# Two graph convolutions and an attention on 200,000 edges: attention by products in the second pass, bf16 parts, and three in-place copies of each one-hot block

## The chip, the core and the metric

The program runs on one core of a Trainium2 chip. A core has five engines that this text names: TensorE (PE: matmuls; PEld: its weight loads), VectorE (DVE), ScalarE (ACT), GpSimd (POOL, which issues the indirect DMAs, here gathers of rows by an index) and SyncE (SP, which issues plain DMAs). Each takes its own instructions strictly in order; they wait for each other by semaphores. The metric is the device time of one execution in microseconds (us). The kernel before takes 4932.1 us, the median of 23 runs from 4896.84 to 4955.6.

## What is computed

Cut to what matters (x is 12500 x 256, src and dst have 200,000 entries, dst is sorted):

```python
def _gcn_conv(x, W, b, src, dst, n):          # src, dst with a loop per node
    h = x @ W
    deg = segment_sum(ones, dst); dinv = rsqrt(deg)
    msgs = h[src] * (dinv[src] * dinv[dst])[:, None]
    return segment_sum(msgs, dst, num_segments=n) + b

def gcn(x):
    h = x @ W_pre + b_pre
    h = relu(_gcn_conv(h, W1, b1)); h = relu(_gcn_conv(h, W2, b2))
    return h @ W_post + b_post

def attention(x):                             # 4 heads x 64
    xt = (x @ weight).reshape(-1, 4, 64)
    alpha_l = einsum('ehd,hd->eh', xt[row], attn_l)
    alpha_r = einsum('ehd,hd->eh', xt[col], attn_r)
    alpha = softmax(leaky_relu(alpha_l + alpha_r, 0.01), axis=1)
    tmp = einsum('nh,nhd->nd', alpha[:n], xt[col[:n]])
    return broadcast tmp over the 4 heads     # n x 256

x = x + gcn(relu(layernorm(x)))
x = x + attention(relu(layernorm(x)))
```

The attention uses only the first 12500 edges (alpha[:n]), and as dst is sorted their targets are the first nodes of the graph (the first 9 windows of 128 nodes), while their sources may be any node.

## The kernel before

A general path for other inputs is not taken here. The fast path has four stages: preparation (to about 132 us: layer norm, degrees, the scaled table of rows in DRAM, table1), pass 1 and pass 2 over all edges, one for each graph convolution, and the attention's tail (from 4717 us). Nodes are in 98 windows of 128. Edges are in 112 chunks of 14 tiles of 128 edges, 1563 tiles in all.

Both passes are one function, `convolve` (L1153), called at L1437 over table1 and at L1597 over table2. For each tile:

- GpSimd gathers 128 source rows of 256 f32 values from the table into a slot of a chunk's buffer (L1374, `fgot`). Pass 1 has buffers for five chunks (the first four chunks of pass 1 need no gather), pass 2 for four. The buffer is free when the last product of the chunk that used it has ended.
- The one-hot block of the tile, 128 edges x 128 places of the target (`fhot`), is made by VectorE for a whole chunk, one chunk ahead (L1241).
- TensorE adds one-hot transposed times rows to the chunk's accumulator in PSUM (L1382, `facc`). One f32 product is two records in the profile.

When a chunk's last tile has been issued, `close` copies the accumulator by ScalarE (L1276, `fsums`), and schedules two steps: `turn`, eight tiles on, transposes the sums (L1206, `fturn`), and `add`, thirteen tiles on, adds them by VectorE to a sliding buffer of nodes at an offset read from memory (L1293, `buf`). When a window of 128 nodes is complete, `add` schedules the window's own steps. Their order is written out by hand: `at(t, step)` puts a step into a list with the tile after which it is issued, and `run(t)`, called after each tile, issues what is due. So the order on each engine is that of the program, and a step stands behind every tile's instructions issued before it.

A window's steps in pass 1 (`finish1`): a product with the weights (L1417, L1418, six tiles on), and ScalarE's relu to `fo` (L1422, ten tiles on), which is then stored to table2 by a DMA that ScalarE issues (L1423). In pass 2 (`finish2`): two products (`fpz`, L1472; `fpo`, L1488) with relu `fz` (L1482) between; the residual and the statistics of the second layer norm (L1493 to L1504; `sc`, L1501); the normalised rows `h` (L1509), their transposes (L1514, `fpt`), the copy `ht` (L1518), the product with the attention's weights (L1527, `fpx`) and its copy `fxa` (L1535). Parts of this are stored to small tables: `table_l`, `table_e` (left scores) and `table_r` (right rows of the first nine windows); the residual is kept in `kept_x`.

The tail mixes the attention's result for 98 tiles of 128 edges in groups of seven: a gather of left scores for each tile (L1662, `fal`), the right rows by one-hot products (L1652, `fends`), copied by ScalarE (L1654), products for scores not yet in a table (L1633, `lacks`), a softmax over the four heads on VectorE and ScalarE (L1666 to L1678), the weighted sum of heads (L1685 to L1692), and the addition to the kept rows (L1694, `fres`), stored to the output.

Of the kernel before, what the change touches and what calls it, by code (L numbers as in the profile page):

```python
# [17 lines left out]
P = 128  # L18
# [395 lines left out]
def fast_path(  # L414
# [57 lines left out]
    table2 = dram.tile([NT * P, D], F32, name="ftable2")  # L472
    kept_x = dram.tile([NT * P, D], F32, name="kept_x")
# [3 lines left out]
    assert AC * J == NT and AC * CE <= E and XW < NT  # L477
    table_r = dram.tile([XW * P, DR], F32, name="table_r")
    table_l = dram.tile([NT * P, H], F32, name="table_l")

    LW = 3
    table_e = dram.tile([NT * P, H], F32, name="table_e")
# [18 lines left out]
    base_b = const.tile([P, NCH], F32, name="base_b")  # L501
    row_i = const.tile([P, AC], I32, name="row_i")
# [88 lines left out]
    with tc.tile_pool(name="fprep", bufs=1) as prep:  # L591
# [233 lines left out]
        with tc.tile_pool(name="fpsum", bufs=2, space=PSUM) as psum, \  # L825
# [227 lines left out]
            wide = prep.tile([NCH, P], F32, name="wide")  # L1053
            nc.vector.tensor_copy(wide, base.to_broadcast([NCH, P]))
# [7 lines left out]
            nc.tensor.matmul(fk[:, 2, :NCH], wide, ident[:NCH, :NCH], start=True, stop=True)  # L1062
# [7 lines left out]
            for f in after:  # L1070
                f()
            after = [raw_block(ends, m, psum.tile([P, 4 * P], F32, name="ft"), j0)
                     for j0 in (8, 12)]
            nc.vector.tensor_copy(base_b, fk[:, 2, :NCH])
            nc.vector.tensor_scalar(row_i, base_b[:, :AC], lane, float(XW * P - 1), op0=ALU.add,
                                    op1=ALU.min)
# [16 lines left out]
    def check_chunks(work, psum):  # L1093
# [20 lines left out]
        kept = work.tile([1, 1], F32, name="n_kept", bufs=1)  # L1114
        nc.vector.tensor_reduce(kept, pt[:1, 2, :NCH], AX.X, ALU.add)
        nc.vector.tensor_add(kept, kept, counted)
        nc.vector.tensor_scalar(bad_row, kept, -1.0, float(NCH + 1), op0=ALU.mult, op1=ALU.add)
# [12 lines left out]
    def load_late(pool):  # L1130

        nc.scalar.dma_start(roots, root_t)
        for t, w in ((wb, w2), (wo, w_post), (wg[:, :, :D], w_gat)):
            nc.scalar.dma_start(t, w.rearrange("(k p) n -> p k n", p=P))
        nc.scalar.dma_start(b2c, b2.rearrange("(k p) -> p k", p=P))
        nc.scalar.dma_start(bob, b_post.partition_broadcast(P))
        attn = []
        for a in (attn_r, attn_l):
            ar = pool.tile([P, D], F32, name="far", bufs=2)
            nc.scalar.dma_start(ar, a.rearrange("h c -> (h c)").partition_broadcast(P))  # L1140
            attn.append(ar)
        return attn

    def late_weights(pool, attn):

        for i, ar in enumerate(attn):
            for k in range(KC):
                prod = pool.tile([P, H, C], F32, name="fprod", bufs=1)
                nc.vector.tensor_mul(prod.rearrange("p h c -> p (h c)"), wg[:, k, :D], ar)
                nc.vector.tensor_reduce(wg[:, k, D + i * H:D + (i + 1) * H], prod, AX.X,  # L1150
                                        ALU.add)

    def convolve(ep, table, stride, width, ahead, with_sum, psum, prepare, finish, lacking=False,  # L1153
                 raw=(), rows_p=None):
# [28 lines left out]
        def run(now=None):  # L1183

            while due:
# [3 lines left out]
                do(d)  # L1189

# [41 lines left out]
        const_p = psum.tile([P, P if with_sum else P + D], F32, name="iota_p", bufs=1)  # L1232
        iota_p = const_p[:, :P]
        nc.vector.tensor_copy(iota_p, iota_w)
        if not with_sum:
            state["bias"] = const_p[:, P:]
            nc.vector.tensor_copy(state["bias"], bob)

# [4 lines left out]

        def hot_of(c):

            n = nj[c]
            h = ep.tile([P, J, P], F32, name="fhot", bufs=3)
# [3 lines left out]
        def new_rows_of():  # L1251
            if with_sum:
                return new_got()
            return rows_p.tile([P, J, stride], F32, name="fgot", bufs=ahead)

        def late_sums():

            h = ep.tile([P, J, P], F32, name="fhot", bufs=3)
# [5 lines left out]
            px = psum.tile([P, KC, P], F32, name="fpt", bufs=1)  # L1264
# [75 lines left out]

        tiles = [(c, j) for c in range(NCH) for j in range(nj[c])]
# [23 lines left out]
        for t, (c, j) in enumerate(tiles):  # L1365
# [7 lines left out]
            if c >= len(raw):  # L1373
                nc.gpsimd.indirect_dma_start(  # L1374
                    out=got, out_offset=None, in_=table[:(NT - TW) * P, :] if some else table[:],
# [4 lines left out]
            if j == (5 if some else 2) and c + 1 < NCH:  # L1380
                hots[c + 1] = hot_of(c + 1)
            nc.tensor.matmul(acc, hots[c][:, j, :], got[:, :width], start=(j == 0),  # L1382
                             stop=(j == nj[c] - 1 and not some))
# [6 lines left out]
            if c + 1 < len(raw):  # L1390
                raw_ahead(c + 1, j)
            run(t)
        run()


# [14 lines left out]
    def finish1(work, psum, w, buf, sbuf, fs):  # L1410
# [9 lines left out]
        def e():  # L1420
            o = work.tile([P, D], F32, name="fo", bufs=3)
            nc.scalar.activation(o, v["po"], AF.Relu, scale=dinv2[:, w:w + 1])  # L1422
            nc.scalar.dma_start(table2[w * P:(w + 1) * P, :], o)  # L1423
            if w == 8:
                late_weights(late, attn)
                first_chunk()
            if w == 9:
                check_chunks(late, psum)

        return [(6, d, fills(w, "fpo")), (10, e, None)]  # L1430

    with tc.tile_pool(name="psum1", bufs=1, space=PSUM) as psum, \
# [6 lines left out]
                 rows_p=late)  # L1439
    ring.close()  # L1440

    ap = ctx.enter_context(tc.tile_pool(name="fatt", bufs=2))
    rows = [ap.tile([P, DR], F32, name="rows", bufs=AC) for c in range(AC)]
    EARLY = 2

    FROM = 40
    assert J % G == 0 and FROM > XW + 2 and FROM + J < NT - LW
    lates = {w: ap.tile([P, DA], F32, name="fxl", bufs=LW) for w in range(NT - LW, NT)}
    early = [ap.tile([P, G, DR], F32, name="fxe", bufs=J // G) for g in range(J // G)]
    hot_l = [ap.tile([P, CE], F32, name="hot_l", bufs=LW) for i in range(LW)]  # L1450

    def prepare2(work, w):
# [6 lines left out]
        nc.sync.dma_start(xb[:n, :], x[w * P:w * P + n, :])  # L1461
        return rb, xb

    def finish2(work, psum, w, buf, pre, bias):
        v = {"root": pre[0], "x": pre[1]}

        def d():
            pz = in_psum(psum, w, "fpz", [P, D], "facc", [P, D], 2)
# [16 lines left out]
        def f():  # L1485
            po = v["po"] = in_psum(psum, w, "fpo", [P, D], "facc", [P, D], 2)
# [4 lines left out]
        def g():  # L1491
# [9 lines left out]
            nc.scalar.activation(v["sc"], mv[:, 1:2], AF.Sqrt, bias=eps)  # L1501

# [8 lines left out]
        def i():  # L1511
            pt = v["pt2"] = in_psum(psum, w, "fpt", [P, KC, P], "fturn", [P, 2 * KC, P])
            for k in range(KC):
                nc.tensor.transpose(pt[:, k, :], v["h"][:, k * P:(k + 1) * P], ident)  # L1514

        def k():
            v["ht"] = work.tile([P, KC, P], F32, name="ht2")
            nc.scalar.activation(v["ht"], v["pt2"][:, :KC, :], AF.Copy)  # L1518
# [4 lines left out]
        def q():  # L1523
            px = in_psum(psum, w, "fpx", [P, DA], "iota_p", [P, P + D])
            px = v["px"] = px[:, d0:] if w + 1 < NT else px[:, :H]
# [4 lines left out]
        def r():  # L1530
            if w < NT - LW:
                xa = work.tile([P, DA], F32, name="fxa")
            else:
                xa = lates[w]
            nc.scalar.activation(xa[:, d0:], v["px"], AF.Copy)  # L1535
            nc.scalar.dma_start(table_l[w * P:(w + 1) * P, :], xa[:, DR:])
            if w < NT - LW:
                nc.scalar.dma_start(table_e[w * P:(w + 1) * P, :], xa[:, DR:])
            if w < XW:
                nc.scalar.dma_start(table_r[w * P:(w + 1) * P, :], xa[:, :DR])  # L1540

        steps = [(6, d, fills(w, "fpz")), (8, e, None), (12, f, fills(w, "fpo")), (14, g, None),
                 (16, h, None), (20, i, fills(w, "fpt")), (22, k, None),
                 (26, q, fills(w, "fpx")), (28, r, None)]
        t = w - FROM
        if 0 <= t < J:

            if t == 0:
                own_rows(0)

            def ends():
                px = v["ends"] = in_psum(psum, w, "fpx", [P, DA], None, None)[:, :DR]
                nc.tensor.matmul(px, hot_t[0][:, t * P:(t + 1) * P], rows[0], start=True,
                                 stop=True)

            def copied():
                nc.scalar.activation(early[t // G][:, t % G, :], v["ends"], AF.Copy)

            steps += [(32, ends, "fpx"), (34, copied, None)]
        return steps  # L1560


    hot_t = {}

    def load_ends(pool, c, bufs):
        to_all = pool.tile([P, CE], I32, name="to_all", bufs=bufs)
        nc.sync.dma_start(to_all, dst[c * CE:(c + 1) * CE].partition_broadcast(P))
        return to_all

    def turn_hots(pool, c, to_all, bufs):  # L1570
        hot_t[c] = pool.tile([P, CE], F32, name="hot_t", bufs=bufs)
        nc.vector.tensor_scalar(hot_t[c], to_all, base_b[:, c:c + 1], lane,  # L1572
                                op0=ALU.subtract, op1=ALU.is_equal)

    def own_rows(c):

        nc.gpsimd.indirect_dma_start(
            out=rows[c], out_offset=None, in_=table_r[:],
            in_offset=bass.IndirectOffsetOnAxis(ap=row_i[:, c:c + 1], axis=0))

    with tc.tile_pool(name="psum2", bufs=1, space=PSUM) as psum, \
            tc.tile_pool(name="fwork2", bufs=2) as work, \
            tc.tile_pool(name="edges2", bufs=1) as ep, \
            tc.tile_pool(name="fgots2", bufs=1) as rows_p:
        ep.tile([P, 320], F32, name="apart")
        for c in range(EARLY):
# [166 lines left out]
```

## Time and profile before

| | |
|---|---|
| median of 23 runs | 4932.1 us (4896.84 to 4955.6) |
| the profiled execution | 4923.27 us |
| its span | 4921.3 us |
| TensorE, matmul records | 2709.2 us, 55% |
| TensorE, weight loads | 2070.9 us, 42% |
| VectorE | 1140.6 us, 23% |
| ScalarE | 487.8 us, 10%, 1233 instructions |
| GpSimd | 3111.0 us, 63% |
| DMA by GpSimd's queue | 414.16 MB |
| granted TensorE clock, mean | 0.72 |
| gathers of pass 1 | from 131.9 to some 2345 us |
| gathers of pass 2 | from some 2352 to 4667 us |
| first gather of the tail | 4717.87 us |

The times in the profile are of the one profiled execution. A group's line gives the source line, the engine, the operation, the tiles written and read, the shape and the number of instructions; then their busy time and the mean in ns of one; then the idle time of the engine just ahead of them, with what ended it. "issue" is a wait for nothing that the profile shows, "remote" a semaphore whose sender the profile does not name; for `fsums` and `buf` it is TensorE's. The ends of matmul records are modelled; when a product has really ended is seen by those who waited for it. The granted clock is 1.00 at full speed.

### The profile page before, as it was taken

How to read it: one execution, taken by the hardware profiler on the slowest of the kernel's cores; microseconds unless marked ns; L12 is line 12 of the kernel's file. 1: busy time of each engine (PE TensorE's matmuls, PEld its weight loads, DVE VectorE, ACT ScalarE, POOL GpSimd, SP SyncE). 2: the span in 40 equal slices, each digit the busy share in tenths (PEclk: the TensorE clock that was granted, in tenths of full speed). 3: DMA queues.
4: the chain of work that ended last, by engine and by line, in shares of the span. 5: the costliest groups of instructions: out<-in, count | busy, mean ns of one | idle time of the engine just before them, and what ended most of it. 6: DMA issues, size and time to landing. Idle time of an engine off the chain costs nothing. (4 is left out here: it accounts for less than half of the span.)

```text
span 4921.3 us, 32267 instructions
## 1 busy us (share of the span) xinstructions
PE 2709.2 (55%) x10600; PEld 2070.9 (42%) x10600; DVE 1140.6 (23%) x2421; ACT 487.8 (10%) x1233; POOL 3111.0 (63%) x3299
## 2 busy tenths in 40 slices
PE   5654555555555565556444555555555555454563
PEld 4533333334433443334343444444444444444441
DVE  7412111111111111112221222222222222221236
ACT  5200000000000000000000100010111001100121
POOL 7566666666666666665666666666666666666633
PEclk7767676667666776767677777777777777777766
DMA  9433333333333333333334433344444444443434
GB/s 278 130 104 99 104 105 102 104 105 108 103 104 104 104 106 104 104 104 94 119 105 108 118 106 103 105 114 109 107 107 114 107 107 110 110 110 102 113 110 153
DMA packets 327420, 554.57 MB, mean 113 GB/s; under 512 B 96302, under 2 KB 224837, under 8 KB 327245
## 3 DMA queue, kind: packets, MB, share of 16 engines
q0 software_dynamic: 153520, 414.16, 31.2%
q1 hardware_dynamic: 127878, 121.99, 8.1%
q10 hardware_dynamic: 45846, 16.27, 1.3%
q8 instruction: 87, 1.43, 0.1%
q14 instruction: 89, 0.72, 0.1%
HBM read 498.89 MB, written 53.21 MB: 112 GB/s over the span
## 5 line engine op out<-in xcount | busy, mean ns | idle before, releaser
L1374 POOL DMA_INDIRECT fgot<-ftable,fsrc_t x3056 | 2899.3, 949 | 1594.2 <-issue 896.2
L1382 PE MATMUL facc<-fgot,fhot 128*128 128x257 f32 (+1 forms) x6252 | 1863.6, 439 | 614.0 <-issue 573.3
L1382 PEld LDWEIGHTS facc<-fgot,fhot 128*128 128x128 f32 x6252 | 1344.0, 222 | 976.0 <-issue 758.5
L1293 DVE TENSOR_TENSOR buf<-buf,fturn 128x256 f32 x224 | 94.5, 422 | 2033.5 <-remote 1253.0
L1241 DVE TENSOR_TENSOR fhot<-iota_p,to_t 128x1792 f32<-128x1792 f32 x224 | 448.9, 2004 | 14.9 <-PE fpt L1267 14.9
L1514 PE MATMUL fpt<-fident,h 128*128 128x128 f32 x194 | 60.1, 408 | 607.0 <-ACT h L1509 583.4
L1514 PEld LDWEIGHTS fpt<-fident,h 128*128 128x128 f32 x194 | 27.1, 188 | 645.4 <-ACT h L1509 617.5
L1488 PE MATMUL fpo<-fwo,fz 128*128 128x256 f32 x388 | 122.2, 443 | 236.6 <-ACT fz L1482 133.9
L1417 PE MATMUL fpo<-wf,buf 128*128 128x256 f32 x388 | 139.0, 495 | 190.8 <-DVE buf L1293 130.8
L1479 DVE SCALAR_TENSOR_TENSOR fy<-rb,fb2c,fpz 128x128 f32<-128x128 f32 x194 | 58.8, 344 | 770.8 <-remote 419.1
L1276 ACT ACTIVATE fsums<-facc 128x257 f32<-128x257 f32 (+1 forms) x224 | 85.6, 382 | 1450.6 <-remote 1213.7
L1493 DVE SCALAR_TENSOR_TENSOR fx<-fpo,fdinv,fxb 128x256 f32<-128x256 f32 x97 | 46.9, 484 | 690.8 <-remote 398.2
L1417 PEld LDWEIGHTS fpo<-wf,buf 128*128 128x128 f32 x388 | 95.6, 253 | 229.7 <-issue 112.5
L1488 PEld LDWEIGHTS fpo<-fwo,fz 128*128 128x128 f32 x388 | 75.6, 214 | 250.7 <-ACT fz L1482 169.1
L1206 PE MATMUL fturn<-fident,fsums 128*128 128x128 f32 x448 | 107.1, 328 | 129.9 <-ACT fsums L1276 109.1
L1472 PE MATMUL fpz<-buf,fwb 128*128 128x128 f32 x776 | 159.2, 374 | 29.9 <-DVE buf L1293 18.6
L1472 PEld LDWEIGHTS fpz<-buf,fwb 128*128 128x128 f32 x776 | 151.0, 287 | 34.6 <-DVE buf L1293 21.9
L1206 PEld LDWEIGHTS fturn<-fident,fsums 128*128 128x128 f32 x448 | 72.5, 172 | 185.8 <-ACT fsums L1276 131.3
L1422 ACT ACTIVATE fo<-fpo,fdinv 128x256 f32<-128x256 f32 x97 | 46.0, 474 | 940.8 <-remote 785.0
L1527 PE MATMUL fpx<-fwg,ht 128*128 128x4 f32 (+1 forms) x388 | 61.6, 267 | 117.4 <-issue 65.0
L1662 POOL DMA_INDIRECT fal<-table_l,fsrc_t x84 | 80.5, 958 | 68.3 <-DVE fs L1669 43.6
L1527 PEld LDWEIGHTS fpx<-fwg,ht 128*128 128x128 f32 x388 | 63.2, 206 | 130.9 <-issue 69.0
(267 smaller groups left out, 1810.0 us busy)
## 6 DMA issues: line engine op xcount, KB each, us to landing
fgot<-ftable,fsrc_t POOLq DMA_INDIRECT x3056
self<-ftable SPq DMA_DIRECT2D x99, 128.0 KB
self<-ftable SPq DMA_DIRECT2D x97, 130.0 KB
ftable<-fo ACTq DMA_DIRECT2D x98, 128.0 KB
kept_x<-fx SPq DMA_DIRECT2D x98, 128.0 KB
fxb<-in_x_dram SPq DMA_DIRECT2D x97, 128.0 KB
fxr<-kept_x SPq DMA_DIRECT2D x13, 896.0 KB
out_dram<-fres SPq DMA_DIRECT2D x13, 896.0 KB
```

The source lines that it names most:

```text
L1206: nc.tensor.transpose(v["pt"][:, i * KC + k, :], rows[:, k * P:(k + 1) * P], ident)
L1241: nc.vector.tensor_tensor(h, iota_p[:, None, :].to_broadcast([P, n, P]), to[:, :, None].to_broadcast([P, n, P]), ALU.is_equal)
L1276: nc.scalar.activation(sb, acc, AF.Copy)
L1293: nc.vector.tensor_add(b, b, v["pt"][:, :KC, :])
L1374: nc.gpsimd.indirect_dma_start(out=got, out_offset=None, in_=table[:(NT - TW) * P, :] if some else table[:], in_offset=bass.IndirectOffset ...
L1382: nc.tensor.matmul(acc, hots[c][:, j, :], got[:, :width], start=(j == 0), stop=(j == nj[c] - 1 and not some))
L1417: nc.tensor.matmul(po, buf[:, k, :P], wf[:, k, :], start=(k == 0), stop=False)
L1472: nc.tensor.matmul(pz[:, m, :], wb[:, k, m * P:(m + 1) * P], buf[:, k, :P], start=(k == 0), stop=(k == KC - 1))
L1488: nc.tensor.matmul(po, v["z"][:, m, :], wo[:, m, :], start=(m == 0), stop=(m == KC - 1))
L1514: nc.tensor.transpose(pt[:, k, :], v["h"][:, k * P:(k + 1) * P], ident)
L1527: nc.tensor.matmul(px, v["ht"][:, k, :], wg[:, k, d0:], start=(k == 0), stop=(k == KC - 1))
L1662: nc.gpsimd.indirect_dma_start(out=al[:, i, :], out_offset=None, in_=(table_l if c else table_e)[:], in_offset=bass.IndirectOffsetOnAxis(a ...
```

## The change

Four things are changed.

1. Ahead of each gathered tile's product, ScalarE copies the tile's one-hot block onto itself three times (`spread`), in both passes, except for the first four chunks of pass 1 and for the last chunk of both.
2. Pass 1 stores each window's result a second time, as three bf16 parts whose sum is the f32 value (`parts2`, 1536 bytes a row). Pass 2 gathers rows of parts, its one-hot blocks are bf16, and a tile has three bf16 products in place of one in f32. Pass 2 has gather buffers for three chunks, not four.
3. The attention moves into pass 2. `feed` takes parts of it from a list of items when the windows that they need are done, and schedules them between the tiles. Left scores come from one-hot products with the scores of all windows done so far, in five stages of windows (`alpha_l`), right scores and rows from a load at an offset read from memory (`ends_of_tile`, 98 loads on SP) and products (`alpha_r`); then the softmax, and the mix as a product (`group`, 14 groups). The rows of indices that the one-hots compare with are loaded broadcast to 128 partitions. Edges whose source lies in windows 84 to 97 are late: pass 1 lists them (`list_late`), up to 16 blocks of 128, and pass 2 prepares their one-hots and right rows (`late_hots`, `late_ends`).
4. The tail has neither the 98 gathers of `fal` nor the products and mixes of groups. For the 16 blocks of late edges it gathers kept rows (16 gathers), makes scores by products, a softmax and a mix, and writes the results with 16 indirect stores to the output.

The core of the diff:

```diff
+        def feed(t):
+            if behind and t >= free_at[0] and behind[0][0]():
+                _, space, parts = behind.pop(0)
+                for i, part in enumerate(parts):
+                    if part:
+                        at(t + i, lambda _, part=part: part())
+                free_at[0] = t + space
...
+        hot_type = F32 if parts is None else BF16
...
-            return rows_p.tile([P, J, stride], F32, name="fgot", bufs=ahead)
+            return rows_p.tile([P, J, 3 * stride], BF16, name="fgot", bufs=ahead)
...
+        def spread(h):
+            for _ in range(3):
+                nc.scalar.activation(h, h, AF.Copy)
...
             if c >= len(raw):
+                rows_of = table if parts is None else parts
                 nc.gpsimd.indirect_dma_start(
-                    out=got, out_offset=None, in_=table[:(NT - TW) * P, :] if some else table[:],
+                    out=got, out_offset=None,
+                    in_=rows_of[:(NT - TW) * P, :] if some else rows_of[:],
...
-            nc.tensor.matmul(acc, hots[c][:, j, :], got[:, :width], start=(j == 0),
-                             stop=(j == nj[c] - 1 and not some))
+            if len(raw) <= c < NCH - 1:
+                spread(hots[c][:, j, :])
+            many = 1 if parts is None else 3
+            for i in range(many):
+                nc.tensor.matmul(acc, hots[c][:, j, :], got[:, i * width:(i + 1) * width],
+                                 start=(j == 0 and i == 0),
+                                 stop=(j == nj[c] - 1 and i == many - 1 and not some))
...
+            feed(t)
             run(t)
...
         def e():
-            o = work.tile([P, D], F32, name="fo", bufs=3)
-            nc.scalar.activation(o, v["po"], AF.Relu, scale=dinv2[:, w:w + 1])
+            po = v["po"]
+            nc.scalar.activation(po, po, AF.Relu, scale=dinv2[:, w:w + 1])
+            v["parts"] = work.tile([P, 3, D], BF16, name="fparts", bufs=2)
+            nc.scalar.activation(v["parts"][:, 0, :], po, AF.Copy)
+            o = work.tile([P, D], F32, name="fo", bufs=2)
+            nc.scalar.activation(o, po, AF.Copy)
             nc.scalar.dma_start(table2[w * P:(w + 1) * P, :], o)
+
+        def split():
+            po, b = v["po"], v["parts"]
+            nc.vector.tensor_tensor(po, po, b[:, 0, :], ALU.subtract)
+            nc.vector.tensor_copy(b[:, 1, :], po)
+            nc.vector.tensor_tensor(b[:, 2, :], po, b[:, 1, :], ALU.subtract)
+            nc.sync.dma_start(parts2[w * P:(w + 1) * P, :], b.rearrange("p i d -> p (i d)"))
...
+            def mix():
+                v["p"] = bank()[:, :G * C].rearrange("p (t c) -> p t c", c=C)
+                for j in range(G):
+                    nc.tensor.matmul(v["p"][:, j, :], v["w"][:, j * P:(j + 1) * P],
+                                     ends[:, b * G + j, :C], start=True, stop=True)
...
+        for t in range(0, NT, G):
+            items.append((when("w", XW), G, [lambda t=t + i: ends_of_tile(t) for i in range(G)]))
+        for b in range(NG):
+            items.append((when("w", XW), 4, alpha_r(b)))
+        for b in range(KL // 4):
+            items.append((when("w", XW), 6, late_hots(b)))
+        for k in range(KL):
+            items.append((when("w", XW), 4, late_ends(k)))
+        for s in range(len(STAGES) - 1):
+            for b in range(NG):
+                items.append((when("w", STAGES[s][1]), 4, alpha_l(s, b)))
+        for b in range(NG):
+            items.append((when("w", LATE), 8, group(b)))
...
+                nc.gpsimd.indirect_dma_start(
+                    out=out[:], out_offset=bass.IndirectOffsetOnAxis(ap=late_i[:, 0, i:i + 1],
+                                                                     axis=0),
+                    in_=sets["x"][:, i, :], in_offset=None)
```

## Prediction

> **What bounds the kernel now.** I read the table of stages first (pass 1 from 196 to 2330 us, pass 2 from 2420 to 4640), because the page's shares mix four stages. Columns: the stretch, its length, busy us of each engine with instructions, the granted TensorE clock, the DMA share, GB/s.
>
> ```profile
> 196.00:2330.00 2134.00, 1227.75 (x4196) 852.93 (x4194) 360.32 (x663) 117.10 (x264) 1393.49 (x1470) 0.70 0.37 103
> 2420.00:4640.00 2220.00, 1174.83 (x5055) 989.83 (x5054) 486.11 (x1033) 222.88 (x598) 1420.73 (x1499) 0.74 0.41 108
> ```
>
> No engine is full, ScalarE (the fourth busy figure) least of all: 5% and 10%. So the next view is the groups on the page and GpSimd's waits:
>
> ```profile
> L1374 POOL DMA_INDIRECT fgot<-ftable,fsrc_t x3056 | 2899.3, 949 | 1594.2 <-issue 896.2
> L1382 PE MATMUL facc<-fgot,fhot 128*128 128x257 f32 (+1 forms) x6252 | 1863.6, 439 | 614.0 <-issue 573.3
> L1276 ACT ACTIVATE fsums<-facc 128x257 f32<-128x257 f32 (+1 forms) x224 | 85.6, 382 | 1450.6 <-remote 1213.7
> ```
>
> ```profile
> POOL fgot L1374 <- issue: 900.1, 2910, 12.2
> POOL fgot L1374 <- remote: 503.1, 134, 5.7
> POOL fgot L1374 <- PE facc L1382: 174.8, 20, 10.9
> ```
>
> A gather costs GpSimd 0.95 us and 0.30 of issue: 1.25 us, 17.5 us for a chunk of 14. The last two lines, 678 us, are waits for a free gather buffer, which TensorE's last product of an old chunk gives. Over 218 chunks that is 3.1 us each. From the starts of the gathers a chunk takes 20.0 us in pass 1 and 20.6 in pass 2: **GpSimd's floor of 17.5 plus 2.5 to 3.1 for TensorE**, which holds three or four chunks of gathered, unread rows all the time. The pace is TensorE's. The timeline of pass 2 shows one period (start, us, what, idle time before it):
>
> ```profile
> 3724.66 0.38 ACT L1276 ACTIVATE fsums<-facc 128x256 f32<-128x256 f32 x1 [7.69 <-remote]
> 3725.59 0.69 PE L1514 MATMUL fpt<-fident,h 128*128 128x128 f32 x2 [7.91 <-ACT h L1509]
> ...
> 3736.98 1.03 PE L1382 MATMUL facc<-fgot,fhot 128*128 128x256 f32 x4
> ...
> 3741.18 0.94 POOL L1374 DMA_INDIRECT fgot<-ftable,fsrc_t  x1 [0.30 <-issue]
> 3744.85 0.38 ACT L1276 ACTIVATE fsums<-facc 128x256 f32<-128x256 f32 x1 [7.68 <-remote]
> 3745.08 0.94 POOL L1374 DMA_INDIRECT fgot<-ftable,fsrc_t  x1 [2.96 <-remote]
> ```
>
> TensorE records its last product of the chunk by 3738.0, but the copy that needs only that product starts at 3744.85, 6.9 us later, and the next gather with it. So the records run ahead of the completions when products come densely. In pass 1 the same is seen with a burst, then a crawl:
>
> ```profile
> 1028.14 6.23 PE L1382 MATMUL facc<-fgot,fhot 128*128 128x257 f32 x28
> ...
> 1040.24 0.38 PE L1382 MATMUL facc<-fgot,fhot 128*128 128x257 f32 x1 [0.83 <-issue]
> ...
> 1041.65 0.49 PE L1382 MATMUL facc<-fgot,fhot 128*128 128x257 f32 x1 [1.03 <-issue]
> ```
>
> Fourteen tiles (two records each) in 6.23 us, 0.44 us a tile; twelve us later one record takes 1.4 us, though the rows lie ready. Why it crawls the trace does not say.
>
> **The change, part by part. 1. Copies of one-hot columns.** 107 chunks of pass 1 and 111 of pass 2, 14 tiles, three copies: 9156 ScalarE instructions. Price of one 128x128 copy: the 128x28 row (L980) is 216 ns and the 128x256 row (L1482) 417, so 304 ns between them; three are 0.91, and since each waits for the one before, I take 0.95 us a tile. Lower bound 0.64, if they overlap by the 0.09 us seen between fsums (3724.66 + 0.38) and h (3724.95); upper bound 1.25 (three of 417 ns). The bf16 copies of pass 2 have the same element count and no row; between half and the same, I take the same. So 13.3 us a chunk. Nothing hides them: the copies of chunk c+1 stand behind fsums of chunk c on ScalarE, fsums waits for the last product of c, and the first product of c+1 waits for the third copy. Where TensorE had work for three chunks in hand, it now has one tile. The loop of a chunk is: the copies, ScalarE's other work, the wait from the last copy to fsums. Other work in pass 1: 117.10 us over 107 chunks is 1.1; the new finish adds two copies (0.42 each, 0.875 windows a chunk) 0.7, its DMA issue (0.35) 0.3: 15.4 us in all. Pass 2: 222.88 over 108 is 2.1, DMA issues 0.9, attention copies 0.7 (some 75 us): 17.0. The wait is bounded by 1.3 us (one tile at the slower 0.86 us of two 0.43 us records, and a hop of 0.4) and by the 6.9 us above. **I take 4.1, the middle**, as neither row fits: products 0.95 us apart are less dense than those that ran 6.9 late, but TensorE crawls in pass 1. That gives 19.5 us in pass 1 (16.7, so GpSimd's 17.5, to 22.3) and 21.1 in pass 2 (18.3 to 23.9): 107 x -0.5 = **-54 us** (-268 to +246) and 111 x 0.5 = **+55** (-255 to +366). ScalarE becomes the engine that is busiest, and what stands behind a copy on it (relu, fz, h, ht: each 2 to 4 tiles after its products) is late by up to a tile, which the hand-set steps have room for.
>
> The Trainium skill ("ScalarE: Activation LUTs", What ACT_TABLE_LOAD costs) gives an activation without operands 186 ns and 0.833 ns an element, 293 ns here, and its table puts plain copies on VectorE; by that the copies are 12.3 us a chunk instead of 13.3. The trace speaks more loudly on another rule of it, "TensorE: Matmul & The Clock Gate" (Why this matters for your kernels): no idle gaps over some 3 us, or the clock is halved. Spaced products would keep that rule, and if the clock were all, both passes would fall to rival A; but here clock 0.70 is granted to a TensorE that always has unread rows, so idle gaps for want of data are not what halves it.
>
> **2. Three bf16 parts.** In pass 1 two more ScalarE copies a window (counted), three VectorE operations (some 0.4 us each by L1293's 422 ns, on an engine 17% busy: hidden) and a 192 KB store on SP. In pass 2 the gathers carry 1536 B a row instead of 1024: 0.41 of the DMA time becomes at most 0.41 x 1.5 = 0.61, still covered; GpSimd's 1.25 us depends on the row count by the one row there is, no row shows other sizes, so between 1.25 and 1.5 times that, I take the same. TensorE issues three products of 256 columns instead of two records of the f32 product; between half and 1.5 times the 0.88 us of those; it stands in the shadow of the copies at 0.95 unless it is slow. Three gather buffers instead of four: two chunks ahead are 35 us, over a whole period, so nothing. Cover gone: see D.
>
> **3. Attention in pass 2.** Some 900 small products (317 to 568 ns by L1633 and L1652: about 350 us over 2220, TensorE's records at 53%), VectorE about 300 us (22% to 35%), and 98 row loads and wide broadcasts on SP. They run behind the windows' steps, beside a ScalarE that sets the pace: nothing, beyond the 0.7 us counted; up to +1.5 us a chunk in the last 30, 45 us, if products and copies meet. The lists of late edges in pass 1: some 20 small products at L1633's 0.32 us are 6 us if nothing hides them; I take 5.
>
> **4. The tail.** Now the first gather of the attention is at 4717.9 and the end at 4921.3: 203 us.
>
> ```profile
> L1662 POOL DMA_INDIRECT fal<-table_l,fsrc_t x84 | 80.5, 958 | 68.3 <-DVE fs L1669 43.6 <-issue 24.4 <-DVE fm L1674 0.3
> L1652 PE MATMUL fends<-rows,hot_t 128*128 128x260 f32 x168 | 70.4, 568 | 82.4 <-issue 40.5 <-ACT fxg L1654 39.0 <-ACT fs L1673 2.5
> L1694 DVE TENSOR_TENSOR fres<-fxr,fmix 128x1792 f32<-128x1792 f32 (+2 forms) x15 | 28.4, 1896 | 0.5
> ```
>
> All three groups leave it. What is left is the late edges: 16 products and a softmax (some 10 us), the first mix (three passes over 1024 elements at L1694's 1.06 ns: 3 us), 16 scatters at a gather's 1.25 us (20 us, the other mixes beside them), landings and the last gathers of kept_x (10): 45 us, between 30 and 80. **-158 us** (-173 to -123).
>
> **Sum.** 4923.3 (the profiled execution, span 4921.3) - 54 + 55 + 5 - 158 = 4771; the median of the runs is 8.8 above that execution, so **4780 us**.
>
> **The rivals.**
> A: even spacing cures the crawl, completions follow at 1.3 us, and GpSimd's floor holds: 17.5 and 18.3 us, 4923 - 268 - 255 + 5 - 158 + 9 = 4256; with half of it in hand, 4500. For: bursts precede the crawl. Against: in pass 2 a period without a crawl is no shorter. Chance 0.20.
> C, the forecast: 4620 to 4940. Chance 0.38.
> B, slower: the wait from last copy to fsums stays near 6.9 us, because TensorE is slow while gathers stream whatever the spacing (it completes 2.9 to 5.5 us after GpSimd has stopped), and it can no longer make up for it at 0.44 us a tile. From 5.0 us on, pass 1 at 20.4 and pass 2 at 22.0, it eats the tail's gain (107 x 0.4 + 111 x 1.4 = 198 us); at 6.9: 4923 + 246 + 366 + 5 - 158 + 9 = 5390; typically 5150. Chance 0.29.
> D, slower: the wider gathers set pass 2. At 1.2 times 1.25 us a chunk takes 21 us, where it starts to decide; at 1.4 times 24.5: 111 x 3.9 = 433, so 4923 - 54 + 433 + 5 - 158 + 9 = 5160. Chance 0.13.
> That the copies do not hold the products (ScalarE runs far ahead, pace as before) is excluded beyond one chunk by fsums; it would give C's time.
>
> **How the numbers follow.** Faster by over 0.2% (what a measurement of this kernel can tell): A's 0.20 and 0.31 of C, 0.51; within 0.2%: 0.03 of C; slower: 0.29, 0.13 and 0.04 of C, 0.46. The range leaves out A's best and the ends of B: 4390 to 5300; C's own is 4620 to 4940.
>
> **What would show it.** ScalarE at 60 to 70% busy; copies of 128x128 near 304 ns, 0.95 us a tile; fsums followed at once by copies and GpSimd waiting 2 to 4 us a chunk; completions 1 to 7 us after a chunk's last copy; gathers of 1536 B at 0.95 us; the end some 60 us after the last product. Wrong is this if chunks take 17.5 us (A), if the wait before fsums is 6 us or more (B), if the gather's mean grows past 1.2 us (D), or if tail and passes overlap differently.

## The result, and the profile after

The changed kernel takes **5662.7 us** (median of 8 runs, 5655.5 to 5667.9) beside 4932.2 for the kernel before: 1.148 times as long, 95% interval 1.1456 to 1.1505. Forecast were 4780 us, in a range from 4390 to 5300. The sign was wrong and the range too narrow. The profiled execution has a span of 5681.8 us.

First the table of stages of the kernel after, cut at its own passes (columns as before):

```profile
134.00:2443.00 2309.00, 1417.42 (x4413) 829.87 (x4414) 547.05 (x1136) 1384.47 (x4844) 1423.73 (x1506) 0.73 0.38 108
2505.00:5548.00 3043.00, 1718.77 (x8357) 1179.27 (x8357) 783.06 (x1613) 1511.79 (x5312) 1477.67 (x1563) 0.66 0.47 134
```

From its first gather to its last, pass 1 takes 2309.2 us (before 2189.5, from 131.9 to 2321.4), pass 2 3042.8 (before 2313.7); from pass 2's last gather to the end are 134.1 (before 255.4). The spans differ by 760 us: pass 1 +120, the gap between the passes +31, **pass 2 +729**, the tail -121, and 2 us ahead of the first gather. A chunk of 14 gathers has 21.5 us in pass 1 and 27.3 in pass 2 (before 20.3 and 20.7). ScalarE (the fourth busy figure) is busy 60% of pass 1 and only 50% of pass 2: its own work, 12.9 us a chunk in pass 1 and 13.5 in pass 2, is not what fills the 27 us.

The groups of the page, then TensorE's waits in pass 1 and in pass 2 (us in all, times, longest):

```profile
L1417 PE MATMUL facc<-fgot,fhot 128*128 128x256 bf16 (+1 forms) x7815 | 2292.2, 430 | 2120.1 <-ACT fhot L1368 1864.6
L1368 ACT ACTIVATE fhot<-fhot 128x128 f32<-128x128 f32 (+1 forms) x9156 | 2566.3, 304 | 544.4 <-ACT fhot L1368 129.8
L1404 POOL DMA_INDIRECT fgot<-parts,fsrc_t x1549 | 1465.2, 946 | 1561.4 <-PE facc L1417 1058.1
```

```profile
PE facc L1417 <- ACT fhot L1368: 736.4, 409, 8.9
```

```profile
PE facc L1417 <- ACT fhot L1368: 1108.9, 458, 13.7
PE facc L1417 <- issue: 106.0, 80, 9.9
```

The releaser of the products has changed. Before, TensorE waited for "issue", with rows lying ready; now the product waits for the copy of its own one-hot block, up to 13.7 us at once. The copy is as cheap as was forecast (304 ns), and the gather of 1536 B a row costs what one of 1024 did (946 ns). So the next view is what ScalarE itself waits for, first in pass 2:

```profile
ACT l_all L1833 <- remote: 228.4, 46, 7.7
ACT sc L1799 <- DVE mv L1797: 224.0, 88, 9.2
ACT fz L1780 <- issue: 209.4, 59, 12.9
ACT ht L1817 <- remote: 163.4, 18, 13.2
ACT fz L1780 <- DVE fy L1777: 154.8, 32, 15.9
ACT fsums L1301 <- PE facc L1417: 92.7, 106, 4.0
```

Not fsums, to which the prediction gave the wait of the loop, but the window's other steps: l_all (the score copy), sc, fz and ht, 980 us in these five lines without fsums. Pass 1 is another case. Its window step (fpo) hardly waits:

```profile
ACT fsums L1301 <- PE facc L1417: 146.3, 76, 6.2
ACT fsums L1301 <- remote: 139.1, 27, 7.6
ACT fhot L1368 <- ACT fhot L1368: 124.6, 163, 1.6
ACT buf L1340 <- DVE buf L1318: 124.0, 21, 7.7
ACT fhot L1368 <- issue: 107.6, 153, 2.3
ACT fhot L1368 <- remote: 99.0, 54, 2.4
ACT fpo L1464 <- remote: 14.6, 3, 5.8
```

There fsums waits 285 us (2.7 a chunk) and the copies themselves 331 (3.1 a chunk). One period of pass 2 shows how a late step stops the products:

```profile
3728.33 1.53 ACT L1368 ACTIVATE fhot<-fhot 128x128 bf16<-128x128 bf16 x5
3728.77 0.85 PE L1825 MATMUL fY<-fwg,ht 128*128 128x4 f32 x4
...
3731.33 1.49 PE L1417 MATMUL facc<-fgot,fhot 128*128 128x256 bf16 x6
...
3735.00 0.17 ACT L1833 ACTIVATE l_all<-fY 128x4 f32<-128x4 f32 x1 [5.14 <-remote]
3735.06 0.48 DVE L1791 SCALAR_TENSOR_TENSOR fx<-fX,fdinv,fxb 128x256 f32<-128x256 f32 x1 [10.61 <-remote]
...
3736.26 0.29 ACT L1799 ACTIVATE sc<-mv,feps 128x1 f32<-128x1 f32 x1 [1.08 <-DVE mv L1797]
...
3736.46 0.97 ACT L1368 ACTIVATE fhot<-fhot 128x128 bf16<-128x128 bf16 x3
...
3737.49 0.82 PE L1417 MATMUL facc<-fgot,fhot 128*128 128x256 bf16 x3 [4.68 <-ACT fhot L1368]
3738.35 0.38 ACT L1301 ACTIVATE fsums<-facc 128x256 f32<-128x256 f32 x1 [0.91 <-PE facc L1417]
3738.59 0.94 POOL L1404 DMA_INDIRECT fgot<-parts,fsrc_t  x1 [6.39 <-PE facc L1417]
```

TensorE records the product of the score step (fY) by 3729.6; the copy that needs it starts at 3735.00. Until then ScalarE, which works in order, makes no copy; the last tile's copies come at 3736.46, behind sc, which waits for VectorE; the tile's product at 3737.49; and GpSimd, out of buffers, has waited 6.39 us. Before the change no gathered tile's product needed anything that stood behind such a step.

### The profile page after: what moved, and what is told of

Same layout as the page of the kernel before. It is cut to its first block, busy times and chain, and to the rows that moved or that the text cites. A ratio compares the mean times of both kernels' runs of the same rounds, so it can differ in the third digit from the quotient of the medians.

```text
span 5681.8 us, 49839 instructions
## 1 busy us (share of the span) xinstructions
PE 3319.3 (58%) x13647; PEld 2142.1 (38%) x13647; DVE 1489.5 (26%) x3189; ACT 3043.2 (54%) x10585; POOL 3031.1 (53%) x3226
## 5 line engine op out<-in xcount | busy, mean ns | idle before, releaser
L1417 PE MATMUL facc<-fgot,fhot 128*128 128x256 bf16 (+1 forms) x7815 | 2292.2, 430 | 2120.1 <-ACT fhot L1368 1864.6
L1368 ACT ACTIVATE fhot<-fhot 128x128 f32<-128x128 f32 (+1 forms) x9156 | 2566.3, 304 | 544.4 <-ACT fhot L1368 129.8
L1404 POOL DMA_INDIRECT fgot<-parts,fsrc_t x1549 | 1465.2, 946 | 1561.4 <-PE facc L1417 1058.1
L1404 POOL DMA_INDIRECT fgot<-ftable,fsrc_t x1507 | 1424.7, 945 | 892.1 <-issue 432.4
L1417 PEld LDWEIGHTS facc<-fgot,fhot 128*128 128x128 f32 x3126 | 628.2, 243 | 1384.1 <-ACT fhot L1368 1165.6
L1417 PEld LDWEIGHTS <-fhot 128*128 128x128 bf16 x4689 | 491.4, 123 | 1746.1 <-ACT fhot L1368 1449.4
L1263 DVE TENSOR_TENSOR fhot<-iota_p,to_t 128x1792 f32<-128x1792 f32 (+1 forms) x224 | 449.0, 2004 | 12.2 <-remote 12.2
L1989 PE MATMUL behind<-l_all,hot_s 128*128 128x72 f32 (+1 forms) x980 | 178.1, 354 | 32.3 <-DVE hot_s L1888 17.5
L1989 PEld LDWEIGHTS behind<-l_all,hot_s 128*128 128x128 f32 x980 | 174.1, 273 | 39.9 <-issue 35.1
L1770 PE MATMUL fX<-buf,fwb 128*128 128x128 f32 x776 | 160.7, 376 | 2.9 <-issue 2.9
```

Source lines behind the costliest of these rows:

```text
L1263: nc.vector.tensor_tensor(h, iota_p[:, None, :].to_broadcast([P, n, P]), to[:, :, None].to_broadcast([P, n, P]), ALU.is_equal)
L1368: nc.scalar.activation(h, h, AF.Copy)
L1404: nc.gpsimd.indirect_dma_start(out=got, out_offset=None, in_=rows_of[:(NT - TW) * P, :] if some else rows_of[:], in_offset=bass.IndirectOf ...
L1417: nc.tensor.matmul(acc, hots[c][:, j, :], got[:, i * width:(i + 1) * width], start=(j == 0 and i == 0), stop=(j == nj[c] - 1 and i == many ...
L1770: nc.tensor.matmul(pz[:, m, :], wb[:, k, m * P:(m + 1) * P], buf[:, k, :P], start=(k == 0), stop=(k == KC - 1))
L1989: nc.tensor.matmul(v["p"][:, j, :, :], v["h"][:, j * P:(j + 1) * P], l_all[:, w0:w1, :], start=True, stop=True)
```

## The experiments

Three theories. **W**: the copies have put ScalarE's in-order waits into the path of the products; each step on it that waits for a completion now holds the next products, which makes the next completions later. **L**: what pass 2 was given besides (wider gathers, three products a tile, the attention's items) is slow by itself. **S**: the copies cost what ScalarE's time for them is.

One thing must be known to read the numbers: the experiments ran on six chips, and the kernel before takes 4150 to 4153 us on five of them and 4902 on the other. Each time is given beside the kernel before on the same chip, and compared with it.

**1. No copies, one copy, copies ahead; the kernel before with copies.**

```diff
-            if len(raw) <= c < NCH - 1:
-                spread(hots[c][:, j, :])
```

> The changed kernel without the copies of one-hot blocks, all else kept. Theory W (the copies put ScalarE's in-order waits into the products' path: every step on ScalarE that waits for TensorE or VectorE now holds the next products): both passes go back to about 20 to 21 us a chunk and the shorter tail stays, so 4750 to 4900 us. Theory L (pass 2 is slow because of what it was given besides: gathers of 1536 B, three products a tile, the attention's items): pass 1 goes back to 20 us, pass 2 stays at 26 us or more a chunk, 5450 us or more. Theory S (the copies cost what their ScalarE time is): 4750 to 4900 as well; told from W by the next runs.

```diff
+            if len(raw) <= c < NCH - 1:
+                for _ in range(3):
+                    nc.scalar.activation(hots[c][:, j, :], hots[c][:, j, :], AF.Copy)
             nc.tensor.matmul(acc, hots[c][:, j, :], got[:, :width], start=(j == 0),
```

> The kernel before with the three copies ahead of each gathered product in both passes, nothing else. W: pass 2 slows by 3 us a chunk or more, as its window steps have five ScalarE steps that wait (relu, sc, h, ht, fxa), pass 1 by about 1 us: 5350 to 5650 us. L: pass 1 as in the changed kernel (21.3 us), pass 2 at most 21.5: 5050 to 5150 us.

```diff
-            if len(raw) <= c < NCH - 1:
-                spread(hots[c][:, j, :])
+            while spread_to < min(t + 9, len(tiles)) and tiles[spread_to][0] in hots:
+                c1, j1 = tiles[spread_to]
+                if len(raw) <= c1 < NCH - 1:
+                    spread(hots[c1][:, j1, :])
+                spread_to += 1
```

> The changed kernel with each block's three copies issued eight tiles before its product, so the same ScalarE work, but a wait on ScalarE no longer holds the next product at once. W: most of the loss goes, 4800 to 5050 us. L: as the changed kernel, 5600 to 5700. S: as the changed kernel, since ScalarE has the same work.

```diff
-            for _ in range(3):
+            for _ in range(1):
```

> The changed kernel with one copy in place of three: ScalarE has 8.5 us a chunk less to do, and keeps every wait. W: the waits stay, only part of the loss goes: 5000 to 5400 us. S: two thirds of the loss over the kernel without copies goes: about 5100. L: 5500 or more.

Measured: 4169.0, 4194.1, 4168.8 and 4179.8 us, beside 4152.9 for the kernel before (ratios 1.0031, 1.0095, 1.0044, 1.0070; intervals at most 0.0017 to either side). All four expectations missed, since the chip was one where most chunks take 17.5 us, GpSimd's own pace. Copies ahead cost nothing there (S would have them cost as much as copies in place, for which see part 2). The kernel before with copies has 17.6 and 17.5 us a chunk in its passes; its 41 us more lie nearly all behind the last gather (204 us, against 165 in the profile of part 3), and why they lie there was not looked into.

**2. The changed kernel, and two of the four again, on one chip.**

> The changed kernel as it is. The kernel before took 4153 us in the runs beside the last four experiments, not 4932: there every kernel stood at GpSimd's 17.5 us a chunk, with or without copies. Theory W says that the copies cost only where TensorE's completions come late; so beside a kernel before at about 4150 us this one takes 4180 to 4250, beside one at about 4930 it takes 5600 to 5700.

> The changed kernel without the copies, once more. Beside a kernel before at 4930 us: W 4750 to 4900 us, L 5450 us or more. Beside one at 4150 us: 4170.

> The changed kernel with the copies eight tiles ahead, once more. Beside a kernel before at 4930 us: W 4800 to 5050 us, L and S 5600 to 5700. Beside one at 4150: 4170.

Measured: the changed kernel 4371.2 us, without copies 4159.2, with copies ahead 4168.6, beside 4149.8 (ratios 1.0531, interval 1.0500 to 1.0561; 1.0027, 1.0016 to 1.0039; 1.0041, 1.0022 to 1.0061). So in place the copies cost 212 us, and the same copies, with the same ScalarE work, cost 9 when they are issued eight tiles earlier. One copy in place (part 1, also beside 4150) stood 11 us above the kernel without copies and three stand 212: not in proportion to ScalarE's time. **S falls.** The changed kernel was expected at 4180 to 4250: W had the mechanism but not the size on a chip without late completions. There pass 1 stands at 17.6 us a chunk with copies in place; pass 2 at 19.9 (without copies 18.1).

**3. The kernel before, for its profile, and the copies without the attention's items** (left out: both kinds of scores, softmax and mix of the early edges, so most of the attention's part of the output).

> The kernel before, unchanged, for a profile where it takes about 4150 us. If TensorE's completions come on time there: gathers every 17.5 us a chunk in both passes, GpSimd waiting for TensorE less than 60 us in all, the copy of the sums within 1 us of the chunk's last product record. Where it takes about 4930 instead, the same 20.0 and 20.6 us a chunk as in the first profile.

```diff
-        for t in range(0, NT, G):
-            items.append((when("w", XW), G, [lambda t=t + i: ends_of_tile(t) for i in range(G)]))
-        for b in range(NG):
-            items.append((when("w", XW), 4, alpha_r(b)))
...
-        for s in range(len(STAGES) - 1):
-            for b in range(NG):
-                items.append((when("w", STAGES[s][1]), 4, alpha_l(s, b)))
-        for b in range(NG):
-            items.append((when("w", LATE), 8, group(b)))
-        for t0, n in ((LATE, G), (LATE + G, 4), (LATE + G + 4, 3)):
-            items.append((when("x", t0 + n), 1, rest(t0, n)))
```

> The changed kernel with its copies, but without the attention's items in pass 2 (left out: the right scores, left scores, softmax and mix of the early edges, so most of the attention's part of the output; the lists and the tail of late edges stay). Read from its pass 2, beside 19.9 us a chunk with the items and 18.1 with the items but no copies (both where the kernel before takes 4150). W: the items add waits and TensorE work to the same loop; without them pass 2 takes 17.5 to 18.0 us a chunk, also in the last 14 chunks. L, if the parts and the wider gathers matter: 18.5 or more over the whole pass.

Measured in one run each: 4158.9 and 4097.1 us, beside 4152.0. The kernel before stands at 17.6 us a chunk in both passes, and so do the copies without items, whose last 14 chunks take 17.5. So in place the copies do not slow the passes while the loop has slack, on the chip without late completions, and it is the items that take the slack. In this profile of the kernel before, where the copy of the sums had to wait it starts 0.04 us after the end of TensorE's last record of a gathered product (median; at most 0.90), so there the completions come on time, as was expected. What the kernel before waits for on this chip, GpSimd and then TensorE:

```profile
POOL fgot L1374 <- PE facc L1382: 39.5, 106, 7.1
```

```profile
PE facc L1382 <- DMA fgot<-ftable,fsrc_t: 856.4, 1104, 4.8
```

Here TensorE waits for rows; in the profile of the record the same program had GpSimd wait 678 us for TensorE.

**4. TensorE loaded.** To make TensorE's products end later on a chip where their completions come on time, both kernels got more products, zeros times the gathered rows, added to the same sums (the cut shows the changed kernel; the kernel before got one a tile in both passes).

```diff
+            if c >= len(raw) and j + 1 < nj[c]:
+                for i in ((0,) if parts is None else (0, 1, 2, 0)):
+                    nc.tensor.matmul(acc[:32, :], zeros, got[:, i * width:(i + 1) * width],
+                                     start=False, stop=False)
```

> The kernel before with one more product a tile, zeros (32 columns) times the gathered rows, added to the same sums: TensorE gets some 0.43 us a tile more (a record pair at full clock), 6 us a chunk, so its completions come later. Where the kernel before takes 4150: pass pace between 17.5 and 20 us a chunk, 4200 to 4700 us in all, by both theories.

> The changed kernel with as much more TensorE work (in pass 1 one product of zeros a tile, in pass 2 four in bf16). W: later completions lengthen every wait on ScalarE, and the copies behind it, and the loop closes: pass 2 at 23 us a chunk or more, 4850 to 5500 us, and at least 400 us above the kernel before with the same work. L or S (the loss is a fixed price of pass 2 or of the copies): the same 220 us above it as without the added work, or less.

> The changed kernel with the copies eight tiles ahead and the same added TensorE work. W: most of the loss of the run before is gone, at most 150 us above the kernel before with the same work. S: as the run before.

> The changed kernel without the copies and with the added products of zeros (one in pass 1, four in bf16 in pass 2). The kernel before with such products took 4377 us, the changed kernel 4882, with the copies eight tiles ahead 4328. W: 4280 to 4400, so the 500 us are the copies'. L: 4700 or more, so they are the other parts'.

Measured, all beside 4150 to 4152 us (the last on another chip): the kernel before 4376.5 (ratio 1.0542, 1.0512 to 1.0573), the changed one **4882.2** (1.1760, 1.1726 to 1.1795), copies ahead 4328.4 (1.0427, 1.0396 to 1.0457), no copies 4333.9 (1.0440, 1.0419 to 1.0461). With TensorE loaded, the changed kernel loses 506 us on the kernel before with the same products, while the two versions without copies in place are faster than that one. The load costs the kernel before 227 us and the changed one 511 (against part 2, on another chip of 4150 us). The four times are as W expected, and L falls here; but pass 2 of the loaded changed kernel takes 21.9 us a chunk, where W had 23 or more. What the load does not do is delay the news of an end, which is what the record shows. The copy of the sums of the loaded changed kernel still follows TensorE's last record, which ends at 3520.79, by 0.04 us:

```profile
3520.29 0.50 PE L1419 MATMUL facc<-fgot,fhot 128*128 128x256 bf16 x3 [0.62 <-ACT fhot L1368]
3520.83 0.38 ACT L1301 ACTIVATE fsums<-facc 128x256 f32<-128x256 f32 x1 [0.59 <-PE facc L1419]
```

So this part shows that copies in place cost some 500 us where TensorE has no slack; it does not stand for the late completions of the record, for which see part 6. GpSimd's waits of the loaded changed kernel, and of the one with copies ahead:

```profile
POOL fgot L1406 <- PE facc L1419: 830.1, 200, 80.9
```

```profile
POOL fgot L1407 <- PE facc L1423: 265.5, 97, 74.4
```

**5. The attention's groups further apart**, without copies.

```diff
-            items.append((when("w", LATE), 8, group(b)))
+            items.append((when("w", LATE), 11, group(b)))
```

> The changed kernel without the copies, and with 11 tiles between the starts of the attention's last 14 groups instead of 8. Beside a kernel before at 4150 us, where without this it took 4159 to 4169 and the last 14 chunks 22.9 us each: if the crowding of the groups is what slows the end, those chunks take 19 to 21 us and the whole 4100 to 4140, faster than both kernels; if it is each group's own work, 4150 to 4170. Beside a kernel before at 4930: W 4700 to 4900, L 5400 or more.

Measured: **4136.5 us** beside 4151.6, ratio 0.9966 (0.9952 to 0.9980). The last 14 chunks take 19.1 us each, not 22.9. It is the only whole version that beats both kernels, by 0.3%; it was run only where the kernel before takes 4150.

**6. Where the kernel before takes 4900.** Two versions were run on such a chip, once each.

> The changed kernel without copies. Where the kernel before takes 4930 us: W 4750 to 4950, L 5400 or more. Where it takes 4150: 4160 to 4170, which tells nothing new.

> The changed kernel with the copies eight tiles ahead. Where the kernel before takes 4930 us: W 4800 to 5050, L and S 5600 or more. Where it takes 4150: 4165 to 4180.

Measured: without copies 5149.4 us, copies ahead 5248.0, beside 4901.9. Both lie outside what W and L expected, between them. Pass 2 takes 23.7 and 24.1 us a chunk, 27.3 with copies in place (in the profile of the record), 20.7 in the kernel before. TensorE's wait for copies in pass 2 with copies ahead:

```profile
PE facc L1421 <- ACT fhot L1368: 65.0, 68, 2.7
```

65 us, not 1109, as W has it. In pass 1 TensorE waits for copies nearly as long as with copies in place (736 us):

```profile
PE facc L1421 <- ACT fhot L1368: 555.9, 396, 6.0
```

Yet that pass 1 is only 38 us longer than the one without copies (2236.0 and 2198.2), so the sum of such waits is no price. And W is not all. Without any copies, the first 14 chunks of pass 2, which come before any product of the attention's items, take 20.3 us (before: 21.1), so three bf16 products and wider gathers cost nothing even there, nor do the tiles in PSUM that the window's products now share (`fX`, `fY`). The next 28 take 24.4, the last 14 29.4. Sorted by whether TensorE has products of the items (`behind`) in a chunk, pass 2 shows what is slow (mean us a chunk, number of chunks):

| | no items in the chunk | items in the chunk |
|---|---|---|
| record, before | 20.7 (111) | |
| no copies, beside 4902 | 20.8 (74) | 29.8 (37) |
| copies ahead, beside 4902 | 20.9 (74) | 30.7 (37) |
| record, copies in place | 24.0 (75) | 34.2 (36) |
| no copies, beside 4150 (part 2) | 17.5 (66) | 19.0 (45) |
| copies in place, beside 4150 (part 2) | 17.6 (74) | 24.4 (37) |

So the items are slow on this chip by themselves, 332 us over the 37 chunks. In the record copies in place cost some 3 us a chunk also where there are no items; beside 4150 us they cost only where items are. ScalarE's waits in the pass 2 without any copies are longer than with copies in place; there no gathered tile's product needs ScalarE, so such a sum is no price either:

```profile
ACT l_all L1831 <- remote: 496.0, 43, 16.2
ACT sc L1797 <- DVE mv L1795: 291.8, 73, 29.0
ACT fz L1778 <- DVE fy L1775: 267.1, 35, 29.7
```

Put beside the record (one profile each, the two kernels before within 0.6%): of the 729 us in pass 2, 2649.2 - 2313.7 = 336 are all that is not copies, by the table the attention's items; 2690.7 - 2649.2 = 42 are the copies when issued ahead, and 3042.8 - 2690.7 = 352 their place directly ahead of the product. Of the 120 in pass 1 these are 9, 38 and 73. The split sets runs of one chip beside a record that may be of another.

## Why the prediction was wrong, point by point

- **What bounds the kernel**: right for the profile shown (GpSimd's 17.5 us and a remainder for TensorE), but for the pace: by its own first view, 1470 gathers in 2134 us and 1499 in 2220, a chunk takes 20.3 us in pass 1 and 20.7 in pass 2, not 20.0 and 20.6. That the remainder belongs to the chip the profile could not tell: the same program stands at 17.6 elsewhere. Nor does the density of the products decide whether records run ahead of completions: in the loaded kernels of part 4, at a granted clock of 0.94 to 0.97, the copy of the sums follows by 0.04 us.
- **The copies' price**: right. 304 ns each; a tile's three take 0.98 us from the first start to the last end, and back to back the next tile's three follow after 0.88, where 0.95 was taken. The page of the Trainium skill that the prediction set beside it ("ScalarE: Activation LUTs") gives 293 by its figures, near the 304 measured; but its table of rules names relu, max, min, add and mul for VectorE, not plain copies.
- **The loop of a chunk**: the step that failed. It gave ScalarE's other work its busy time (2.1 us a chunk of pass 2) and one wait, for fsums, of 4.1 us, and said of relu, fz, h and ht that the hand-set steps have room for them to be late. They have room for TensorE and VectorE; but ScalarE waits in order at each, and the copies of the next tiles are behind it. In pass 2 ScalarE was busy 13.5 us a chunk and not busy 13.7 (the DMA issues of its queue among that), where the sum had 17.0 of work and 4.1 of waiting. fsums waited 117 us (92.7 by the line above, 24.2 by another), about 1 us a chunk; l_all, sc, fz and ht 980, 8.8 a chunk, the longer for the items. So pass 2 came to 27.3 us, where 21.1 was taken and 23.9 was the end of the range. In pass 1 the waiting was 8.6 us a chunk and the work 12.9, where 4.1 and 15.4 were taken; its window step had little part in it (the lines above): fsums waited 2.7, less than was taken, and the copies themselves 3.1, for which the sum had no term. That 21.5 lies inside its range of 17.5 to 22.3 is partly luck, since the two misses are of opposite sign.
- **bf16 parts**: right, nothing (the runs of part 6); a gather's issue is 946 ns for 1536 B a row.
- **Attention in pass 2: "nothing, beyond the 0.7 us"**: wrong where completions are late, some 336 us there by part 6, where 45 were the most that was allowed for. Elsewhere the items cost the last chunks: without copies a chunk takes 17.5 us until the groups crowd and 22.9 then, which is 14 x 5.4 = 75 us.
- **The tail**: -158 forecast, -121 measured from the last gather on. Right in kind, 37 us too much, and just outside its -173 to -123.
- **The rivals**: B had the sign and a closed loop, but its wait was the one for fsums, and its time ended at 5390. D's price was wrong (gathers are no slower), A never came: with copies in place 17.5 us a chunk were seen only where the kernel before has them too.
- **The range** summed two passes' bounds from one wait. That a wait on ScalarE makes the next completion later, so that waits add up in a loop, as theory W has it, has no place in such a sum.

On the clock: the rule of the Trainium skill that the prediction weighed ("TensorE: Matmul & The Clock Gate", Why this matters for your kernels: no idle gaps over some 3 us) did not decide the time. The runs agree with it in that a denser TensorE keeps its clock: with more products the granted clock of the kernel before rose to 0.97 (from 0.80), though with this added work it became 227 us slower. And in part 2 the changed kernel with and without copies in place was granted 0.78 in both profiles, 212 us apart. A high clock is here a sign of a busy TensorE, not of a fast kernel.

**What stays open.** Why completions come late on one chip and not on another was not found. There ScalarE's own dependent copies crawl too, beside TensorE, as this stretch of pass 1 of the kernel after shows:

```profile
1516.03 0.31 ACT L1368 ACTIVATE fhot<-fhot 128x128 f32<-128x128 f32 x1 [1.04 <-ACT fhot L1368]
...
1517.41 0.51 ACT L1368 ACTIVATE fhot<-fhot 128x128 f32<-128x128 f32 x2 [1.08 <-ACT fhot L1368]
...
1520.21 0.31 ACT L1368 ACTIVATE fhot<-fhot 128x128 f32<-128x128 f32 x1 [2.29 <-issue]
1520.91 0.31 ACT L1368 ACTIVATE fhot<-fhot 128x128 f32<-128x128 f32 x1 [0.39 <-ACT fhot L1368]
```

Two of these copies wait 1.0 and 1.1 us for the copy before them alone, and one 2.29 us for nothing that the profile shows, where 0.03 is usual. Of the 2996 gaps inside a tile's three copies in this pass 1, 200 are over 0.5 us; in the changed kernel's profile beside 4150 us (part 2) none is. This would fit late news of an end, of ScalarE's as well as of TensorE's; it is not shown, and neither is what would delay it. Nor was it tried to give the attention's items another order on such a chip.

## What to carry to other kernels

An instruction put ahead of a product on an engine that works in order brings all of that engine's waits with it, not only its own time: count, for the engine, each step that waits for somebody, and who is queued behind it. If it must be there, issue it several steps early; the same 9156 copies cost 212 us in place and 9 us eight tiles ahead, where the kernel before takes 4150. And a kernel whose loop has no slack should be tried on more than one chip before a margin of a few per cent is believed.

## What was not expected of the hardware

- The same program took 4150 us on five chips (4147.4 to 4152.2 in 11 runs of one) and 4902 on another, like the 4932 of the record. In the profile of the record a copy of the sums starts 6.9 us after the record of the last product that it needs (the period in the prediction); in the profile of part 3, 0.04 us after it.
- More TensorE work raised its granted clock: 0.80 to 0.97 with one more product a tile.
- Three dependent copies of 128x128 take 0.98 us from the first start to the last end, in f32 and in bf16 alike (median 0.975 for both in the profile of the record).
